# A sixth buffer for the x tiles of the last stage, and two work tiles with one buffer each

## The chip, the cores and the metric

The kernel runs on one core of one Trainium2 chip. The metric is the device time of one execution in microseconds (us), the median over runs. All data is float32.

## What is computed

Two bottleneck blocks of a residual network follow each other on an input of 64 images, 1024 channels, 14 x 14 pixels. Cut to what matters, one block is:

```python
out = relu(bn(conv1x1(x, w1, b1), g1, be1))      # 1024 -> 256 channels
out = relu(bn(conv3x3(out, w2, b2), g2, be2))    # 256 -> 256
out = bn(conv1x1(out, w3, b3), g3, be3)          # 256 -> 1024
out = relu(x + softplus(residual_scale)[0] * out)
```

`bn` takes mean and variance over all images and pixels of a channel, so a block can't be normalized before the whole of its convolution is known. The output of the first block is the `x` of the second.

## The kernel before

The activations between the convolutions (256 channels, all pixels) stay in SBUF as `y_all`. The 1024-channel tensor does not fit: it is cut into T = 32 tiles of two images, `[128, 8, 392]` float32, 1568 KB each, which travel between HBM and SBUF. The second block reads its x tiles from the DRAM tiles `mids`.

The stages run one after the other: first 1x1 convolution of block 0, its 3x3 convolution, a stage that fuses the last convolution of block 0 with the first of block 1, the 3x3 convolution of block 1, the Gram stage (products of `y` with itself, from which the statistics of the last convolution are computed before it runs), and the last stage, `final`. The change lies in the last one.

**The last stage.** Tile 0 is done by `residual` with plain products. Then `final` takes the tiles in pairs, t and t + 1 for t = 1, 3, ..., 29: 15 pairs. Tile 31 is done by `residual` again. A pair is 4 units (`q` = 0 to 3), and each unit makes two slots of 128 output channels for both tiles. A unit is a two by two block product done with seven products instead of eight (`Seven`, `Conv3Pair`): p1 to p7, each one product of a 128 x 128 weight and 392 columns, which the profile shows as two matmul instructions of L175. The sums that this needs of the operands, t1 to t4, are made once a pair by `column_sums` on DVE (L468 makes t3, L469 t2 = t3 + y, L470 t1, L471 t4 = y - t2). In the profile all four are named `ct`, in memory they are the tags ct0 to ct3. t1 is read by p5, t2 by p6, t3 by p7 and t4 by p4. Likewise the weights' sums are `ws`, and the plain weights `w`.

`stream` sets the order on PE. For each unit it issues p1 of this unit, p3 and p4 of the unit before, then p6, p2, p5 and p7 of this unit. So the unit before ends inside this one; at a pair's border p4 of the old pair still reads the old t4 after p1 of the new pair. PE and ACT instructions are held in program order; most of DVE's, POOL's and SP's are placed by the framework's scheduler, which hands out a buffer only when all readers of its former tile are done.

What the products make is drained so:

- p1, p6, p7 and p4 add up in one PSUM bank (`cy`). After p1, p6 and p7 ACT copies the bank's state, scaled, into SBUF (L338, named `cu`: twice into `cu12`, once into `cu3`), and the next product onto the bank waits for that copy.
- DVE adds the banks of p2, p5, p3 and p4 to the x tiles in place (L504). p5 and p3 add up in one bank (`cp`), so p3 waits for the add that follows p5. The add after p2 goes to the first tile of the pair, the one after p5 to the second.
- POOL adds `cu12` (L551, twice a unit) and `cu3` (L525, once a unit) to the x tiles.
- ACT does bias and relu on three of the unit's four parts (L338, `x<-x,shift`), DVE on the fourth (L560), and SP issues two stores for the unit (L563), when two more units have been begun.

Loads are issued by SP too (`load_x`, L129). Five tiles are loaded ahead of the stage: the pool `x_left` has five buffers, some of which serve the Gram stage as `homes` until it is over. In pair t, after its second unit, the loads up to tile t + 4 are requested; each waits until the stores of the tile that had its buffer have landed.

Of the kernel before, what the change touches and what calls it, by code (L numbers as in the profile page):

```python
# [38 lines left out]
FP = mybir.dt.float32  # L39
# [3 lines left out]
P = 128  # L43
# [6 lines left out]
T = N // G  # L50
PX = G * HW
# [39 lines left out]
def bottlenecks(ctx: ExitStack, tc: tile.TileContext, x, w1s, w2s, w3s, pars, out):  # L91
# [14 lines left out]
    def two(t, s):  # L106

        j = t % (GI // G)
        return y_grp[:, s, t // (GI // G), :, j * G * W : (j + 1) * G * W]

    class Psum:


        def __init__(self, scope, cycle, **bufs):
            self.pool = scope.enter_context(
                tc.tile_pool(name="psum", bufs=1, space=bass.MemoryType.PSUM, reuse_waits="tile")
            )
            self.cycle, self.bufs = itertools.cycle(cycle), bufs
# [5 lines left out]
    def load_x(pool, b, t, parts=1, run=lambda ins: None):  # L124
        xt = pool.tile([P, CS, PX], FP, tag="x", name=f"x_{b}_{t}")
        n = CS // parts
        for i in range(parts):
            run(
                nc.sync.dma_start(  # L129
                    out=xt[:, i * n : (i + 1) * n, :].rearrange("p s f -> p (s f)"),  # L130
                    in_=(x[t] if b == 0 else mids[t])[:, i * n * PX : (i + 1) * n * PX],
                )
            )
        return xt
# [12 lines left out]
    def sums_tile(pool, n):  # L147

        return pool.tile([P, n, 4 * CS // 2 * P], FP, tag="ws", name="ws")
# [14 lines left out]
    def combine_w3(w, s):  # L164
        n = CS // 2
        return combine([[w[:, k, o * n : (o + 1) * n] for k in range(MS)] for o in range(2)], s)

    def load_w3(pool, b):
        w = pool.tile([P, MS, CS, P], FP, tag="w3", name=f"w3_{b}")
        nc.sync.dma_start(out=w, in_=w3s[b])  # L170
        return w
# [168 lines left out]
    class Conv1(Seven):  # L340
# [89 lines left out]
        def run(self, ins, o, i):  # L430
            if self.pinned:
                tc.keep_in_program_order(ins)
# [25 lines left out]
        def after7(self):  # L458
            self.result(1, 1, self.p, self.saved("au3"))

    def column_sums(pool, ys, n):

        sums = []
        for i in range(4):
            v = pool.tile([P, n], FP, tag=f"ct{i}", name=f"ct{i}", bufs=2 if i > 1 else 1)
            sums.append(v.rearrange("p (h l) -> p h l", l=G * W))
        t1, t2, t3, t4 = sums
        nc.vector.tensor_sub(t3, ys[1][1], ys[0][1])  # L468
        nc.vector.tensor_add(t2, t3, ys[0][0])  # L469
        nc.vector.tensor_sub(t1, ys[0][1], ys[0][0])  # L470
        nc.vector.tensor_sub(t4, ys[1][0], t2)  # L471
        return sums

    class Conv3(Seven):

        prefix = "c"

        def __init__(self, psum, pool, xt, q, n, ys, sums, w3, aff, to):  # L480
            self.psum, self.pool, self.xt, self.n = psum, pool, xt, n
# [17 lines left out]
        def part(self, row, i):  # L499
            return self.xt[:, self.o[row], i * self.n : (i + 1) * self.n]  # L500
# [20 lines left out]
            self.add(1, 1, self.p)  # L521

        def after7(self):
            u3 = self.saved(self.pool.tile([P, self.n], FP, tag="cu3", name="cu3", bufs=2), 1)
            nc.gpsimd.tensor_add(self.part(1, 1), self.part(1, 1), u3)  # L525

        def after3(self):
# [12 lines left out]

    class Conv3Pair(Conv3):


        def part(self, row, i):
            return self.xt[i][:, self.o[row], :]
# [834 lines left out]
    def final(psum, pool, xpool, xs, a, w3, aff):  # L1380


        units = []

        def pairs():
            for t in range(1, T - 1, 2):
                ys = [[two(t + i, s) for i in range(2)] for s in range(MS)]
                sums = column_sums(pool, ys, PX)
                for q in range(CS // 2):
                    units.append(Conv3Pair(psum, pool, xs[t : t + 2], q, PX, ys, sums, w3, aff, out[t : t + 2]))  # L1390
                    yield units[-1]

                    while len(units) > 2:
                        units.pop(0).go_out()
                    if q == 1:

                        for i in range(len(xs), min(t + 5, T)):
                            xs.append(load_x(xpool, 1, i))

        for _ in stream(pairs(), (T // 2 - 1) * CS // 2):  # L1400
            pass
        for unit in units:
            unit.go_out()
        residual(psum, xs[T - 1], 1, T - 1, a, aff)
# [182 lines left out]
    def right_pool(name):  # L1587

        scope = ExitStack()
        return scope.enter_context(tc.tile_pool(name=name, bufs=2, side="right")), scope  # L1590

    x_right, x_scope = right_pool("first_x_right")
    with tc.tile_pool(name="first", bufs=1) as one, tc.tile_pool(
        name="first_x", bufs=2
    ) as x_left, ExitStack() as scope:
        xpools = x_right, x_left
        psum = Psum(scope, ["ps"], ps=4, ay=2)
# [37 lines left out]
    for b in range(2):  # L1635
        pb = par[b]
        minus_c = keep.tile([P, MS], FP, tag="minus_c", name="minus_c")
        nc.vector.tensor_scalar(minus_c, pb[:, BE2 : BE2 + MS], 0.0, -1.0, ALU.max, ALU.mult)
        stats2 = keep.tile([P, MS, 1 + PARTS, nc.vector.BN_STATS_DIM], FP, tag="stats2", name=f"stats2_{b}")
        with tc.tile_pool(name=f"conv2_{b}", bufs=1, reuse_waits="tile") as pool, ExitStack() as scope:  # L1640
            border.go_on(Psum(scope, ["l"], l=2, m=2), pool, stats2)

        if b == 0:
            x_right, x_scope = right_pool("last_x_right")
        with tc.tile_pool(name=f"last_{b}", bufs=1) as one, tc.tile_pool(
            name=f"last_x_{b}", bufs=2 if b == 0 else 5
        ) as x_left:
            xpools = (x_right, x_left) if b == 0 else (x_left, x_left)
            w3 = load_w3(one, b)
            if b == 0:  # L1650
                w1 = load_w1(one, b + 1, nc.sync)
            aff = affine(aggregate(stats2, 0), pb, G2, BE2)
            with ExitStack() as scope:
                if b == 0:
                    psum = Psum(scope, ["cy", "ay", "cx", "cy", "ay"], cy=2, ay=2)
                else:
                    psum = Psum(scope, ["cy", "cx"], cy=2, cx=2, cp=2)
                with tc.tile_pool(name=f"gram_{b}", bufs=1) as pool:
                    def x_tile(name, t=0):
                        return xpools[t].tile([P, CS * PX], FP, tag="x", name=name)  # L1660


                    ws = sums_tile(one, 2 - b)
                    homes = [x_tile("home"), x_tile("home") if b else ws.rearrange("p i n -> p (i n)"), x_tile("home", 1)]

                    made_c, made_a = [], []
                    beside = {NPX // (CH * P) - 10: lambda: made_c.append(combine_w3(w3, ws[:, 0]))}
                    if b == 0:
                        beside[NPX // (CH * P) - 4] = lambda: made_a.append(combine_w1(w1, ws[:, 1]))
                    grams = gram(psum, pool, homes, aff, minus_c, beside)  # L1670

                    made = [conv3(psum, 0, 0, w3, "cx" if b else "ay")]
                    mv3 = small.tile([P, CS, nc.vector.BN_AGGR_DIM], FP, tag="mv3", name="mv3")
                    conv3_stats(psum, pool, grams, w3, mv3, ("cy", "cp", "cy", "cp" if b else "cx"), homes[2])
                made.append(conv3(psum, 0, 1, w3, "cx" if b else "ay"))
                tags = ("cy", "cp") * 2 if b else ("cy", "cx", "cy")
                made += [conv3(psum, 0, 2 + i, w3, tag) for i, tag in enumerate(tags)]
                if b == 0:
                    psum.cycle = itertools.cycle(["ay", "ay", "cy"])
                aff = affine(mv3, pb, G3, BE3, conv_bias=B3)  # L1680
                for a in aff:
                    nc.vector.tensor_scalar(a, a, sps[b], None, ALU.mult)
                xs = [load_x(xpools[t % 2], b, t, run=tc.keep_in_program_order) for t in range(2 if b == 0 else 5)]
                later = None if b else []
                residual(psum, xs[0], b, 0, w3, aff, made, later)
                weights = made_a + made_c
                with tc.tile_pool(name=f"rest_{b}", bufs=1) as pool:
                    if b == 1:
                        final(psum, pool, x_left, xs, w3, *weights, aff)
                        return  # L1690
                    stats1 = stats_tile(MS, f"stats1_{b + 1}")
                    border = Border(b + 1, stats1, x_scope)
                    fused(psum, pool, xpools, xs, *weights, aff, par[b + 1], stats1, border, later)
# [40 lines left out]
```

## Time and profile before

| what | value |
|---|---|
| median of 3 runs | 1917.84 us (1916.82 to 1920.01) |
| the profiled execution | 1919.44 us |
| its span, first to last instruction | 1917.7 us |
| granted TensorE clock | 1.00 |
| DMA over the span | 213 GB/s |
| DMA from 1825 to 1850 us, inside the last stage | 357 GB/s, busy 0.97 |
| x tile loads of the second block | 32 of 1568 KB, median 8.6 us to landing |
| stores of the last stage | 392 KB mostly, median 5.6 us to landing |

In a row of a group or of the timeline stand the start and the duration, the engine, the line of the kernel, the operation, what it writes and reads by the program's names, and how often. An arrow in brackets tells how long the engine was idle before it and what ended that. PE is TensorE, PEld its weight loads, DVE VectorE, ACT ScalarE, POOL GpSimd, SP the queue that issues most DMAs. In the rows of stretches each engine has its busy time and, in brackets, its instructions; the last three numbers are the granted clock, the DMA busy share and GB/s.

### The profile page before, as it was taken

To read this page: it belongs to the slowest core of one execution; us is meant where nothing else is said; L and a number is where in the kernel's file an instruction comes from. 1 tells how busy PE (TensorE), PEld (TensorE's weight loads), DVE (VectorE), ACT (ScalarE), POOL (GpSimd) and SP (SyncE) were. 2 spreads that over 40 slices of the span, in tenths; PEclk is the share of its full clock that TensorE was granted. 3 is DMA by queue.
4 is the path that set the end of the run, shared out by engine and by line. 5 is a ranking of instruction groups with operands and counts; after the bars stand their busy time and mean duration, and the time that the engine had idled before them with its cause. 6 is when DMAs were issued, how large, how long until landed. Compare 5 with 4: busy or idle time off the path is not lost. (4 is left out here: it accounts for less than half of the span.)

```text
span 1917.7 us, 28725 instructions
## 1 busy us (share of the span) xinstructions
PE 1900.9 (99%) x10232; PEld 1598.3 (83%) x10232; DVE 1542.5 (80%) x2491; ACT 1086.1 (57%) x2160; POOL 572.6 (30%) x682
## 2 busy tenths in 40 slices
PE   9999999999999999999999999999999999999999
PEld 5555557999998899999999999989999986555555
DVE  5787767999998867677777767789999986888786
ACT  2222214677778255555555555557777692666665
POOL 0111100211205133333434334302121141666664
PEclk9999999999999999999999999999999999999999
DMA  7777644887946534444444444358788466899898
GB/s 286 275 248 279 216 155 152 210 215 208 220 165 172 205 147 169 169 173 184 177 173 168 168 173 178 125 180 218 213 208 224 146 162 251 290 327 346 312 338 300
DMA packets 198527, 408.77 MB, mean 213 GB/s; under 512 B 37104, under 2 KB 175024, under 8 KB 181872
## 3 DMA queue, kind: packets, MB, share of 16 engines
q1 hardware_dynamic: 159712, 321.85, 49.1%
q0 software_dynamic: 33056, 34.03, 8.6%
q10 hardware_dynamic: 5616, 51.06, 6.4%
q8 instruction: 81, 1.33, 0.3%
q14 instruction: 62, 0.51, 0.1%
HBM read 263.75 MB, written 115.34 MB: 198 GB/s over the span
## 5 line engine op out<-in xcount | busy, mean ns | idle before, releaser
L338 ACT ACTIVATE cu<-cy,scale 128x196 f32<-128x196 f32 (+1 forms) x552 | 256.3, 473 | 280.9 <-PE cy L175 275.7
L175 PE MATMUL columns<-v,ub 128*128 128x224 f32 (+1 forms) x1536 | 302.3, 338 | 2.0 <-ACT columns L846 1.0
L338 ACT ACTIVATE x<-x,shift 128x392 f32<-128x392 f32 x452 | 255.0, 613 | 72.8 <-POOL x L530 53.6
L175 PEld LDWEIGHTS columns<-v,ub 128*128 128x128 f32 x1536 | 269.0, 188 | 7.4 <-ACT columns L846 2.2
L504 DVE SCALAR_TENSOR_TENSOR x<-cp,scale,x 128x196 f32<-128x196 f32 (+1 forms) x368 | 178.0, 484 | 100.1 <-PE cp L175 96.3
L175 PE MATMUL cy<-ct,ws 128*128 128x196 f32 (+1 forms) x736 | 221.8, 383 | 1.2 <-ACT cu L338 1.2
L175 PE MATMUL ay<-at,ws 128*128 128x196 f32 (+1 forms) x768 | 212.8, 382 | 0.0
L525 POOL TENSOR_TENSOR x<-x,cu 128x196 f32<-128x196 f32 (+1 forms) x184 | 160.1, 870 | 172.8 <-ACT cu L338 163.7
L530 POOL TENSOR_TENSOR x<-x,cu 128x392 f32<-128x392 f32 x124 | 125.9, 1015 | 191.4 <-DVE x L504 191.4
L175 PEld LDWEIGHTS ay<-at,ws 128*128 128x128 f32 x768 | 139.3, 190 | 34.7 <-issue 0.2
L175 PEld LDWEIGHTS cy<-ct,ws 128*128 128x128 f32 x736 | 133.4, 190 | 36.4 <-ACT cu L338 3.7
L175 PE MATMUL l<-diffs,ub 128*128 128x224 f32 (+1 forms) x768 | 149.6, 337 | 0.3 <-ACT sd L1476 0.3
L551 POOL TENSOR_TENSOR x<-x,cu 128x392 f32<-128x392 f32 x120 | 121.9, 1017 | 87.5 <-DVE x L504 69.1
L175 PE MATMUL m<-sums,ua 128*128 128x224 f32 (+1 forms) x752 | 146.0, 336 | 0.2 <-DVE sums L667 0.2
L338 ACT ACTIVATE au<-ay 128x196 f32<-128x196 f32 (+1 forms) x140 | 53.3, 381 | 152.8 <-PE ay L175 150.0
L175 PEld LDWEIGHTS l<-diffs,ub 128*128 128x128 f32 x768 | 134.6, 189 | 1.2 <-ACT sd L1476 0.6
L504 DVE SCALAR_TENSOR_TENSOR x<-cx,scale,x 128x196 f32<-128x196 f32 (+1 forms) x184 | 89.1, 484 | 56.7 <-PE cx L175 56.7
L175 PEld LDWEIGHTS m<-sums,ua 128*128 128x128 f32 x752 | 131.4, 189 | 1.4 <-DVE sums L667 0.8
L175 PE MATMUL cy<-y,w 128*128 128x196 f32 (+1 forms) x408 | 125.3, 393 | 0.0
L175 PE MATMUL cx<-y,w 128*128 128x196 f32 (+1 forms) x400 | 122.7, 392 | 0.0
L175 PE MATMUL cp<-y,ws 128*128 128x196 f32 (+1 forms) x368 | 113.6, 390 | 2.5 <-DVE x L504 2.5
L175 PE MATMUL cy<-ct,w 128*128 128x196 f32 (+1 forms) x368 | 110.9, 383 | 0.5 <-ACT cu L338 0.5
(238 smaller groups left out, 3918.0 us busy)
## 6 DMA issues: line engine op xcount, KB each, us to landing
x<-in_x SPq DMA_DIRECT2D x62, 1568.0 KB, 6.9
ub<-u SPq DMA_DIRECT2D x92, 768.0 KB, 5.3
x<-mid SPq DMA_DIRECT2D x32, 1568.0 KB, 8.6
mid<-x ACTq DMA_DIRECT2D x31, 1568.0 KB, 5.1
out<-x SPq DMA_DIRECT2D x123, 392.0 KB, 5.6
ua<-u SPq DMA_DIRECT2D x92, 256.0 KB, 3.1
u<-y POOLq DMA_DIRECT2D x48, 256.0 KB, 5.5
home<-y SPq DMA_DIRECT2D x70, 96.0 KB, 3.5
```

The source lines that it names most:

```text
L175: tc.keep_in_program_order(nc.tensor.matmul(*args, **kw))
L338: tc.keep_in_program_order(nc.scalar.activation(*args, **kw))
L504: nc.vector.scalar_tensor_tensor(v, bank, self.scale[:, o : o + 1], v, ALU.mult, ALU.add)
L525: nc.gpsimd.tensor_add(self.part(1, 1), self.part(1, 1), u3)
L530: nc.gpsimd.tensor_add(v, v, self.u12)
L551: nc.gpsimd.tensor_add(v, v, self.u12[:, i * self.n : (i + 1) * self.n])
```

## The change

The last stage gets a sixth buffer for x tiles, `last_more`, in the place that the Gram stage has left. The sixth tile (tile 5) is loaded into it ahead of the stage, behind the other five; from then on every sixth tile uses it. In pair t the loads up to tile t + 5 are requested in place of t + 4. To make room, t4 and `cu3` of the last stage have one buffer in place of two (`twice`, `thirds`); t3 keeps two. The fused stage, which uses the same functions, keeps its buffers.

```diff
-    def column_sums(pool, ys, n):
+    def column_sums(pool, ys, n, twice=(2, 3)):
...
-            v = pool.tile([P, n], FP, tag=f"ct{i}", name=f"ct{i}", bufs=2 if i > 1 else 1)
+            v = pool.tile([P, n], FP, tag=f"ct{i}", name=f"ct{i}", bufs=1 + (i in twice))
...
     class Conv3(Seven):
+        thirds = 2
...
-            u3 = self.saved(self.pool.tile([P, self.n], FP, tag="cu3", name="cu3", bufs=2), 1)
+            u3 = self.saved(self.pool.tile([P, self.n], FP, tag="cu3", name="cu3", bufs=self.thirds), 1)
...
     class Conv3Pair(Conv3):
+        thirds = 1
...
     def final(psum, pool, xpool, xs, a, w3, aff):
-                sums = column_sums(pool, ys, PX)
+                sums = column_sums(pool, ys, PX, (2,))
...
-                        for i in range(len(xs), min(t + 5, T)):
-                            xs.append(load_x(xpool, 1, i))
+                        for i in range(len(xs), min(t + len(xpool), T)):
+                            xs.append(load_x(xpool[i % len(xpool)], 1, i))
...
+                if b == 1:
+                    more = scope.enter_context(tc.tile_pool(name="last_more", bufs=1, reuse_waits="tile"))
+                    xs.append(load_x(more, b, len(xs), run=tc.keep_in_program_order))
                 with tc.tile_pool(name=f"rest_{b}", bufs=1) as pool:
                     if b == 1:
-                        final(psum, pool, x_left, xs, w3, *weights, aff)
+                        final(psum, pool, [x_left] * 5 + [more], xs, w3, *weights, aff)
```

## The prediction

> **What bounds the kernel now.** I read the page first, then the stretches of the last stage, the waits of DVE there, the timeline around one wait and around one pair border, and last SP's timeline. The page:
>
> ```profile
> span 1917.7 us, 28725 instructions
> PE 1900.9 (99%) x10232; PEld 1598.3 (83%) x10232; DVE 1542.5 (80%) x2491; ACT 1086.1 (57%) x2160; POOL 572.6 (30%) x682
> ...
> PE 31%; DMA 2%; DVE 1%; ACT 0%; issue 0%; DVEq 0%; SPq 0%; ACTq 0%
> ```
>
> TensorE is full; the change takes no work from it, so it can win only idle PE time, and only in the last stage (from about 1617 us). The stretches say how little that is, and that the transfers are nearly full too:
>
> ```profile
> 1750.00:1775.00 25.00, 25.00 (x76) 13.79 (x75) 21.18 (x33) 16.45 (x32) 16.61 (x17) 1.00 0.98 349
> 1775.00:1800.00 25.00, 23.45 (x71) 13.06 (x70) 18.59 (x29) 15.81 (x31) 15.36 (x15) 1.00 0.87 306
> ```
>
> The second column is PE: 1.55 us are missing after 1775. The waits of DVE from 1634 to 1900 us, and the timeline at the longest, name the cause:
>
> ```profile
> DVE x L504 <- DMA x<-mid: 2.8, 4, 1.6
> ```
>
> ```profile
> 1788.97 0.82 PE L175 MATMUL cp<-ct,ws 128*128 128x392 f32 x2
> ...
> 1790.29 0.82 PE L175 MATMUL cy<-y,w 128*128 128x392 f32 x2
> ...
> 1791.99 0.62 DVE L504 SCALAR_TENSOR_TENSOR x<-cp,scale,x 128x392 f32<-128x392 f32 x1 [1.59 <-DMA x<-mid]
> ...
> 1792.67 0.93 PE L175 MATMUL cp<-y,ws 128*128 128x392 f32 x2 [1.55 <-DVE x L504]
> ```
>
> The add after p5 needs the second x tile of its pair, which has not landed; p3 accumulates on the same bank and waits for the add. SP shows why the tile is late: each group of two loads waits for the stores that free its buffers, and stands in one queue with eight stores.
>
> ```profile
> 1761.80 2.72 SPq L129 DMA_DIRECT2D x<-mid  x2
> 1764.57 17.77 SPq L563 DMA_DIRECT2D out<-x  x8
> 1782.51 1.06 SPq L129 DMA_DIRECT2D x<-mid  x2
> 1783.62 19.20 SPq L563 DMA_DIRECT2D out<-x  x8
> 1803.45 1.35 SPq L129 DMA_DIRECT2D x<-mid  x2
> ```
>
> Load groups come 20.7 and 20.9 us apart here, while PE takes 18.8 us for a pair when it is not held. The group of 1782.51 carries as its first tile the second tile of the very next pair: landed at 1791.8 (the chain of waits has 9.26 us for it), due at 1789.8, where p5 ends.
>
> A second, smaller loss recurs at each pair border, where DVE makes the next pair's operand sums:
>
> ```profile
> 1708.45 0.82 DVE L469 TENSOR_TENSOR ct<-ct,y 128x392 f32<-128x392 f32 x1
> ...
> 1709.31 0.57 DVE L471 TENSOR_TENSOR ct<-y,ct 128x392 f32<-128x392 f32 x1
> ...
> 1711.00 0.93 PE L175 MATMUL cp<-y,ws 128*128 128x392 f32 x2
> ...
> 1711.72 1.37 DVE L470 TENSOR_TENSOR ct<-y 128x392 f32<-128x392 f32 x1
> ...
> 1713.01 0.55 DVE L468 TENSOR_TENSOR ct<-y 128x392 f32<-128x392 f32 x1
> ...
> 1715.09 0.61 DVE L504 SCALAR_TENSOR_TENSOR x<-cp,scale,x 128x392 f32<-128x392 f32 x1
> ...
> 1715.76 0.93 PE L175 MATMUL cp<-y,ws 128*128 128x392 f32 x2
> ```
>
> From 1708.45 to 1716.54 DVE has no idle. Both p3 start late, by 0.12 and 0.04 us, and each costs another 0.105 us since its second weights are then loaded late (second matmul 0.434 us after the first; 0.329 undisturbed): 0.37 us a border, 5.2 us over 14 borders.
>
> **The change, part by part.**
>
> *Sixth x buffer.* No instruction is added; 32 loads stay 32. At pair t the loads still wait for the stores of tiles t-2 and t-1, but bring tiles t+4 and t+5, not t+3 and t+4. Tile t+3 was the one due in the very next pair; now every load has a further pair, 18.8 us. What it removes, as p1-to-p3 start against 0.70 us at an undisturbed border (1715.06 to 1715.76): 2.38 - 0.70 = 1.68 us at 1790; 1810.77 to 1811.89 is 1.12, so 0.42 at 1811; 1867.62 to 1869.05 is 1.43, so 0.73 at 1868. Sum 2.8 us, all on PE's path. The next thing due behind each is the border itself, already counted. Nor should lateness catch up: from the group of 1685.27 to that of 1880.19 ten intervals average 19.5 us, so a group loses 0.7 us a pair against PE, some 8 us over twelve pairs, under the 18.8 gained. Even at 20.9 throughout it would be 25 us, against 18.8 and the 3 us the early groups had in hand; only the last pairs could then stall.
>
> Here a rule stands against the change. The Trainium skill (DMA: Bandwidth & Descriptors, Specifications) gives about 358 GB/s between HBM and a core. A pair moves four tiles of 1.605 MB: 6.42 MB, 17.9 us at that rate, less than PE's 18.8. By it the transfers keep up and a buffer buys nothing: sum 0. The stretch above does move 349 GB/s, so the rate is right; but the trace's intervals of 20.7 and 20.9 us contain waits that no rate has, and I follow the rows: 2.8 us.
>
> *Its early load.* It follows the fifth on SP, which issues at 1607.73, so about 1608.1. Two queued loads land 4.5 to 5 us apart, so about 1619. DMA is 0.19 busy from 1612 to 1618, and no store stands behind it on SP before 1631. If that cover went, tile 0's store (POOL, 1618.58, 5.4 us) would be later by at most one load, 5 us, with nobody waiting for it but tile 6's load. Cost 0. In return the last group has one load less.
>
> *One buffer for cu3.* ACT's next cu3 must wait for POOL's L525. That ends at 1702.92 for a cu3 begun at 1701.26; the next begins at 1705.87, 2.95 us later (3.1 at the border). Cost 0. Without that cover ACT would hold its later reads of the y bank, which p1 and p6 already wait on by fractions of a microsecond, and PE would pay one for one.
>
> *One buffer for t4.* L471, now at 1709.31, may start only when p4 of the old pair's last unit has read the old t4: 1712.59. It is due at the next p4, about 1716.4. Count stays 15, so nothing is added by its own row of 0.57 us; it moves out of the first half of the dense stretch into the second. Worked through: without it the first p3 is on time (gain 0.23); the ops behind it come 0.4 us earlier until L468; then it goes in and the add after p5 is where it was, 1715.1 or 0.1 later. So 0 at the second p3, which sets the border's end; 0 to +0.1 us a border. The new wait is DVE on PE; queued behind are the adds of p3, p4, p2 and p5, for which POOL, ACT and PE wait.
>
> The trace has no L471 in the new place. Nearest row for the price there: L470, two SBUF inputs like it, 1.37 us where POOL was running, against 0.55 for L468 where POOL was idle. The skill's rule (SBUF — State Buffer, SBUF: two separate sides) says a DVE op with two SBUF inputs and a GpSimd op lock each other out, the earlier one for its whole length. POOL runs from 1714.18 to 1716.32. By L471's present row the border costs 0; by the rule, if the L551 of 1714.18 is ahead of it, up to 0.8 us, times 14 = 11 us. From below: were it placed after the add of p5, both p3 would be on time, -0.37 us times 14 = -5.2. I take 0: directly behind p4 it stands ahead of that POOL op.
>
> *Sum.* The profiled execution took 1919.44 us (span 1917.7 and 1.7 around it): 1919.4 - 2.8 = 1916.6. The median of the runs is 1917.84, 1.6 below it; as the stalls follow from an order fixed in the program, I take them to be in those runs too: 1915.0.
>
> **The rivals.**
> *Slower: t4 behind POOL.* If L471 lands after the add of p4 in DVE's order, at about 1714.2, the L551 begun just before holds it for 0.7 to 0.8 us, and the add of p5, with no slack, goes with it: 0.75 times 14 = 10.5, less 2.8: 1925.5. It decides as soon as L471 sits between POOL's first L551 after the border and the add of p5. For: L470's 1.37. Against: p4 ends before that POOL op starts.
> *Faster by more: the border loosens.* L471 lands where the add of p5 no longer waits for it: half to all of 5.2 us more, 1912.4 to 1909.8. For: the first p3 is surely freed. Against: t4 is due by 1716.4, so it can't go far back.
> *Nothing: the lateness returns.* The queue stays the slower one at 20.9 us, late tiles move to later pairs, or the stalls in the runs are smaller than in the profile: 1917 to 1918.
>
> **How the numbers follow.** Likeliest 0.42 (its own range 1913.5 to 1916.6), slower 0.23, faster by more 0.22, nothing 0.13. A difference under 0.2%, 3.8 us, is about what a measurement of this kernel can't tell from none; below 1914.0 counts as faster, above 1921.7 as slower. Faster: 0.22 and 0.11 from the lower edge of the likeliest, 0.33. Slower: 0.23, with 0.01 from the first. The range leaves out the outer tails: 1910 to 1924.
>
> **What would show it.** Right: no wait of DVE L504 for x<-mid after 1634; six loads before the first L563; p3 at borders late by under 0.4 us together; L471 at 0.5 to 0.6 us behind the add of p3. Wrong: L471 at 0.8 us or more with p3 later than now; an ACT wait for POOL L525; a rest of waits for x<-mid in the last pairs.

## The result

Over 21 runs each the changed kernel takes 1915.12 us (1913.89 to 1916.89), the kernel before 1919.38 us (1916.82 to 1921.44) on the same chips: ratio 0.9980, 95% interval 0.9974 to 0.9987, or 4.3 us less. The profiled execution took 1915.46 us, with a span of 1913.7; the one of before, 1919.44 and 1917.7. (Behind the new lines of code the old L504, L525, L551, L560 and L563 are L505, L526, L553, L562 and L565. The edits of some experiments shift them again: there DVE's adds are L509, and a row's operation and names tell what it is.)

The page of the changed kernel: TensorE's work is the same, the span is 4.0 us shorter, and the chain of waits no longer breaks off at transfers of x tiles.

```profile
span 1913.7 us, 28716 instructions
PE 1899.4 (99%) x10232; PEld 1600.8 (84%) x10232; DVE 1542.1 (81%) x2491; ACT 1087.0 (57%) x2160; POOL 581.8 (30%) x682
...
PE 97%; ACT 1%; DVE 1%; issue 0%; DMA 0%; POOL 0%; SPq 0%; DVEq 0%; ACTq 0%; POOLq 0%
```

The waits of DVE from 1634 to 1896 us, all of them: none is for x<-mid.

```profile
DVE x L505 <- PE cp L175: 21.2, 43, 0.7
DVE x L505 <- PE cx L175: 19.6, 29, 0.7
```

In the stretches PE is full where it lacked 1.55 us, and the transfers are as full as in the first of the two stretches before (349 GB/s):

```profile
1750.00:1775.00 25.00, 25.00 (x76) 13.95 (x75) 21.09 (x34) 16.77 (x32) 17.44 (x17) 1.00 0.98 352
1775.00:1800.00 25.00, 25.00 (x77) 14.23 (x76) 20.58 (x32) 17.62 (x34) 17.02 (x16) 1.00 0.99 352
```

SP's timeline: seven issues stand in the first row, the five tiles, the sixth behind them, and tile 6 in the place where tile 5 was; the load groups then come 18 to 19 us apart in this stretch.

```profile
1584.61 40.46 SPq L129 DMA_DIRECT2D x<-mid  x7
...
1764.17 1.29 SPq L129 DMA_DIRECT2D x<-mid  x2
1765.51 16.51 SPq L565 DMA_DIRECT2D out<-x  x8
1782.19 1.32 SPq L129 DMA_DIRECT2D x<-mid  x2
1783.56 17.15 SPq L565 DMA_DIRECT2D out<-x  x8
1800.87 1.05 SPq L129 DMA_DIRECT2D x<-mid  x2
```

And a pair border in the timeline:

```profile
1708.41 0.82 PE L175 MATMUL cx<-y,w 128*128 128x392 f32 x2
1708.61 0.83 DVE L469 TENSOR_TENSOR ct<-ct,y 128x392 f32<-128x392 f32 x1
1709.36 0.61 DVE L505 SCALAR_TENSOR_TENSOR x<-cx,scale,x 128x392 f32<-128x392 f32 x1
...
1711.04 0.82 PE L175 MATMUL cp<-y,ws 128*128 128x392 f32 x2
1711.28 0.55 DVE L470 TENSOR_TENSOR ct<-y 128x392 f32<-128x392 f32 x1
1711.76 1.37 DVE L468 TENSOR_TENSOR ct<-y 128x392 f32<-128x392 f32 x1
1713.05 0.61 DVE L505 SCALAR_TENSOR_TENSOR x<-cp,scale,x 128x392 f32<-128x392 f32 x1
1713.59 0.55 DVE L471 TENSOR_TENSOR ct<-y,ct 128x392 f32<-128x392 f32 x1
1713.74 1.27 POOL L553 TENSOR_TENSOR x<-x,cu 128x392 f32<-128x392 f32 x1 [1.04 <-DVE x L505]
...
1715.13 0.61 DVE L505 SCALAR_TENSOR_TENSOR x<-cp,scale,x 128x392 f32<-128x392 f32 x1
```

L471 now stands behind the add of p3, ahead of the POOL op; that op takes 1.27 us in place of about 1.02, as it waits for L471. The first p3 (1711.04) is on time, 0.66 us behind p1; the second is 0.15 us late. With the late second weights a border costs PE 0.25 us, and did cost 0.37.

**The accounts of PE.** Take the starts of all matmuls of the last stage and sum what each lies later than 0.329 us behind the one before, where it is over 0.03 us. Before: 9.3 us; after: 4.7. Of the first, 2.8 are late loads, 5.1 borders, and 1.4 the stage's beginning and end. Of the second, 0 are late loads, 3.3 borders and 1.4 the ends. That is 4.6 us less; the span won 4.0, since in this execution the stage began 0.65 us later.

### The profile page after: what moved, and what is told of

Same layout as the page of the kernel before. It is cut to its first block, busy times and chain, and to the rows that moved or that the text cites. A ratio compares the mean times of both kernels' runs of the same rounds, so it can differ in the third digit from the quotient of the medians.

```text
span 1913.7 us, 28716 instructions
## 1 busy us (share of the span) xinstructions
PE 1899.4 (99%) x10232; PEld 1600.8 (84%) x10232; DVE 1542.1 (81%) x2491; ACT 1087.0 (57%) x2160; POOL 581.8 (30%) x682
## 4 chain that ended last, share of the span: by engine, by line
PE 97%; ACT 1%; DVE 1%; issue 0%; DMA 0%; POOL 0%; SPq 0%; DVEq 0%; ACTq 0%; POOLq 0%
PE ay L175 18%; PE cy L175 18%; PE columns L175 15%; PE cp L175 12%; PE ap L175 11%; PE m L175 7%; PE l L175 7%; PE cx L175 5%; PE ax L175 4%; PE ps L175 1%; DMA x<-in_x 0%; PE cx L1207 0%; ACT columns L848 0%; PE cy L1207 0%; ACT x L338 0%
## 5 line engine op out<-in xcount | busy, mean ns | idle before, releaser
L505 DVE SCALAR_TENSOR_TENSOR x<-cp,scale,x 128x196 f32<-128x196 f32 (+1 forms) x368 | 178.2, 484 | 96.2 <-PE cp L175 95.0
L526 POOL TENSOR_TENSOR x<-x,cu 128x196 f32<-128x196 f32 (+1 forms) x184 | 165.8, 901 | 172.6 <-ACT cu L338 163.9
L531 POOL TENSOR_TENSOR x<-x,cu 128x392 f32<-128x392 f32 x124 | 125.9, 1015 | 191.2 <-DVE x L505 191.2
L553 POOL TENSOR_TENSOR x<-x,cu 128x392 f32<-128x392 f32 x120 | 125.8, 1049 | 73.7 <-DVE x L505 72.8
L505 DVE SCALAR_TENSOR_TENSOR x<-cx,scale,x 128x196 f32<-128x196 f32 (+1 forms) x184 | 89.0, 484 | 57.0 <-PE cx L175 57.0
```

The lines of the kernel that those rows point to most:

```text
L505: nc.vector.scalar_tensor_tensor(v, bank, self.scale[:, o : o + 1], v, ALU.mult, ALU.add)
L531: nc.gpsimd.tensor_add(v, v, self.u12)
L553: nc.gpsimd.tensor_add(v, v, self.u12[:, i * self.n : (i + 1) * self.n])
```

## The experiments

The theory, formed from these two traces: the gain has two parts. Late loads go because of the sixth buffer (2.8 us in the profiled execution), and borders get cheaper by 0.12 us because L471 moves (1.8 us over the stage). The rivals: the sixth buffer is all of it; the place of L471 doesn't matter, or it could be worse; the lateness is a full queue that no buffer mends.

### The work tiles alone, with five x buffers

```diff
-                if b == 1:
-                    more = scope.enter_context(tc.tile_pool(name="last_more", bufs=1, reuse_waits="tile"))
-                    xs.append(load_x(more, b, len(xs), run=tc.keep_in_program_order))
...
-                        for i in range(len(xs), min(t + len(xpool), T)):
+                        for i in range(len(xs), min(t + 5, T)):
```

> Five x buffers as before, t4 and cu3 with one buffer each. Theory (the change has two parts: late loads 2.8 us, and 0.12 us a border from moving L471): the first p3 of each border is on time, p1 to p3 start 0.66 us there, the second p3 late by some 0.15 us; the waits of DVE for x<-mid stay at 2.8 us or grow to 5, since PE is faster and the loads are not. Time against before: -1.6 us from the borders, 0 to +1.6 back in waits, so 1917.8 to 1919.4 where before is 1919.4. Rival (the sixth buffer is all of it, the borders only look different): both p3 as late as before, 0.37 us a border, time 1919.4.

Measured: 1916.3 us against 1918.8, ratio 0.9989 (0.9980 to 0.9998). The borders are those of the changed kernel: first p3 on time, second 0.15 us late. So the borders' part is real and comes without the buffer. The late loads came back, but smaller than I had expected. The waits of DVE in this kernel:

```profile
DVE x L505 <- DMA x<-mid: 1.3, 3, 0.5
```

At two borders p1 to p3 is 0.40 and 0.54 us longer than at the others: 0.9 us, not 2.8. (At the last border, where the changed kernel loses nothing, p3 and its second weights are late by 0.2 us more: 1.1 us in all.)

### The kernel before, a second trace

No edit.

> The kernel before, a second trace. Theory: the late loads follow from the fixed order on SP, so the waits of DVE for x<-mid come again at 2.8 us, give or take 0.5, at the same three borders. Rival (they are the luck of a run): some other sum, between 0.5 and 4 us, at other borders.

Measured, in this one execution: 1918.5 us. The theory's number fell. Two borders are late, by 0.34 and 0.96 us, 1.3 us in all, at about 1810 and 1867; the one at 1790, with 1.68 the largest of the first trace, is on time. So the lateness is of the place (it comes in the same stretch, at borders that the first trace had too), its size is of the run. The waits list only 0.2 us for x<-mid here, since the largest stands under another name:

```profile
1867.44 0.63 DVE L504 SCALAR_TENSOR_TENSOR x<-cp,scale,x 128x392 f32<-128x392 f32 x1 [0.86 <-PE cy L175]
```

An add of a `cp` bank has nothing to wait for in `cy`, and its tile landed at 1867.22, 0.2 us ahead of it: it is the load.

### cu3 with two buffers again

On the kernel before, with its five x buffers, t4 alone gets one buffer:

```diff
-    def column_sums(pool, ys, n):
+    def column_sums(pool, ys, n, twice=(2, 3)):
...
-            v = pool.tile([P, n], FP, tag=f"ct{i}", name=f"ct{i}", bufs=2 if i > 1 else 1)
+            v = pool.tile([P, n], FP, tag=f"ct{i}", name=f"ct{i}", bufs=1 + (i in twice))
...
-                sums = column_sums(pool, ys, PX)
+                sums = column_sums(pool, ys, PX, (2,))
```

So it differs from the first experiment by cu3 alone.

> Five x buffers, t4 with one buffer, cu3 with two as before: differs from the first experiment by cu3 alone. Theory (ACT never waits for L525, the slack is 3 us): the same as the first experiment, ratio to before 0.999, no wait of ACT cu for POOL in either. Rival (cu3 with one buffer holds ACT now and then): faster than the first experiment by over 1 us.

Measured: 1916.31 us against 1918.26, ratio 0.9992 (0.9983 to 1.0001); the first experiment had 0.9989. ACT waits for no POOL op ahead of a `cu` in either. No cost of the single cu3 shows. Three borders are late in this trace, by 1.6 us together.

### t4 one place later: behind the add of p4

```diff
-        nc.vector.tensor_sub(t4, ys[1][0], t2)
+        fourth = lambda: nc.vector.tensor_sub(t4, ys[1][0], t2)
...
+            later.append(lambda: tc.keep_in_program_order(fourth()))
...
+        def after4(self):
+            super().after4()
+            self.then4()
...
+                    units[-1].then4 = later[0]
```

The old pair's last unit makes t4 of the next pair, behind its add of p4.

> The changed kernel with L471 held behind the add of p4 on DVE, one place later. Theory (POOL and DVE shut each other out, whichever begins first): L471 meets the L553 that POOL has begun and takes 1.2 to 1.4 us in place of 0.55; the add of p5 and the second p3 come 0.7 to 0.8 us later at 14 borders: +10 us on the changed kernel, about 1925. Rival (the place of L471 doesn't matter as long as it is ahead of p4): L471 0.55 us, 1915.

Measured: 1921.85 us against 1918.8, ratio 1.0017 (1.0008 to 1.0026): slower than before, and 6.7 us slower than the changed kernel, with no late load. The timeline at a border:

```profile
1715.43 1.03 POOL L566 TENSOR_TENSOR x<-x,cu 128x392 f32<-128x392 f32 x1 [1.04 <-DVE x L509]
1715.81 1.07 DVE L471 TENSOR_TENSOR ct<-y,ct 128x392 f32<-128x392 f32 x1
1716.80 0.61 DVE L509 SCALAR_TENSOR_TENSOR x<-cx,scale,x 128x392 f32<-128x392 f32 x1
1717.34 0.61 DVE L509 SCALAR_TENSOR_TENSOR x<-cp,scale,x 128x392 f32<-128x392 f32 x1
```

The POOL op is ahead by 0.38 us, and L471 takes 1.07 us in place of 0.55, ending 0.42 us behind it. The second p3 is 0.67 us late, 0.52 more than in the changed kernel; times 13 that is 6.8 us. The slower rival of the prediction was a true mechanism, one place in DVE's order away. I had its price at 0.7 to 0.8 us, since I let L471 meet the POOL op sooner after its start. And it was held for 0.52 us where 0.65 us of the POOL op were left, so a little less than by the rule that the prediction cites.

### t4 behind the add of p5

The same edit, with `after5` of the new pair's first unit.

> The changed kernel with L471 held behind the add of p5. Theory: the second p3 is on time (-0.25 us a border), but L471 waits for POOL's L553 until 1.0 to 1.4 us after its start, and the p4 that reads t4 starts 0.3 to 0.6 us late: +1 to +4 us on the changed kernel, about 1917.5. Rival (t4 is not due so early): p4 on time, -3.3 us, 1911.9.

Measured: 1915.44 us against 1918.8, ratio 0.9984 (0.9975 to 0.9993), the time of the changed kernel. L471 takes 1.12 us, as expected, and the second p3 is on time:

```profile
1714.42 1.12 DVE L471 TENSOR_TENSOR ct<-y,ct 128x392 f32<-128x392 f32 x1
1715.65 0.30 PEld L175 LDWEIGHTS cy<-ct,w 128*128 128x128 f32 x2 [0.58 <-ACT cu L338]
```

The second row is the weight load of p4. The bracket names a copy of ACT's, but at every border the load starts 0.12 us behind L471's end, so it is t4 that it waits for. p4 is late by 0.15 us only, not 0.3 to 0.6: with its late second weights 0.22 us a border, where the changed kernel has 0.25. At the borders next to nothing is won by it: the delay goes from p3 to p4.

### t4 behind the add of p2, in the kernel before

```diff
-        nc.vector.tensor_sub(t4, ys[1][0], t2)
+        with tc.issue_after(behind.ins) if behind is not None else ExitStack():
+            nc.vector.tensor_sub(t4, ys[1][0], t2)
```

with `behind` the add of p2 of the old pair's last unit. Five x buffers, two buffers for t4 and cu3.

> The kernel before, with five x buffers and two buffers for t4 and cu3, but L471 held one place back, behind the add of p2. Theory (the 0.12 us a border that the change won are the start of L471: directly behind L469, whose t2 it reads, it starts 0.86 us after it, where an add that does not read t2 starts after 0.75): with an add between the two the dense chain is 0.1 us shorter and the border costs PE 0.26 us, not 0.37, though L471 stays in the first half: -1.5 us against before. Rival (the gain comes of L471 leaving the first half): the border stays at 0.37 us, no gain.

Measured: 1915.8 us against 1918.26, ratio 0.9986 (0.9976 to 0.9995). L471, here L472, stays in the first half, and the border still gets cheaper, from 0.37 to 0.10 us. So L471 need not leave the first half for the border to get cheaper. The rows show where the gain lies:

```profile
1707.90 0.83 DVE L469 TENSOR_TENSOR ct<-ct,y 128x392 f32<-128x392 f32 x1
1708.65 0.61 DVE L505 SCALAR_TENSOR_TENSOR x<-cx,scale,x 128x392 f32<-128x392 f32 x1
1709.19 0.55 DVE L472 TENSOR_TENSOR ct<-y,ct 128x392 f32<-128x392 f32 x1
1709.66 0.61 DVE L505 SCALAR_TENSOR_TENSOR x<-cp,scale,x 128x392 f32<-128x392 f32 x1
1710.20 0.64 DVE L561 TENSOR_SCALAR x<-x,shift 128x392 f32<-128x392 f32 x1
...
1709.41 1.21 POOL L552 TENSOR_TENSOR x<-x,cu 128x392 f32<-128x392 f32 x1 [1.10 <-DVE x L505]
```

In the kernel before, L469 started at 1708.45, and then:

```profile
1710.56 1.02 POOL L551 TENSOR_TENSOR x<-x,cu 128x392 f32<-128x392 f32 x1 [1.71 <-DVE x L504]
1710.87 0.93 DVE L560 TENSOR_SCALAR x<-x,shift 128x392 f32<-128x392 f32 x1
```

From L469 to L561 it is 2.30 us; before it was 2.42. This 0.12 is the theory's: what comes next starts 0.75 us behind L469 when it does not read its result, 0.86 when it does. (That the next op is a sum and not an add isn't the reason: L472 starts 0.54 us behind an add, as the add at 1710.33 in the kernel before did behind another, 0.53.) The rest is more than I had expected: L561 takes 0.64 us and not 0.93, as POOL began its op earlier (the add of p2, which releases it, comes 0.6 us sooner after L469), so less of it is left to wait for. The late loads in this trace are 2.2 us, late second weights counted in.

### t3 out of the border

t3 of the next pair is made in the middle of the pair instead of at the border, on the changed kernel:

```diff
+        def third_of(t):
+            v = pool.tile([P, PX], FP, tag="ct2", name="ct2", bufs=2)
...
+            tc.keep_in_program_order(nc.vector.tensor_sub(v, two(t + 1, 1), two(t + 1, 0)))
...
                     if q == 1:
+                        third = third_of(t + 2) if t + 2 < T - 1 else None
```

> The changed kernel with t3 of the next pair (L468, 1.37 us at the border because POOL runs) made in the middle of the pair, behind the DVE instruction that follows its second unit's request. Theory (what is left of the border is DVE's dense chain): both p3 on time, PE loses nothing at the border: 0.25 us by 13 is -3.3 us, 1911.9. Rival (the wait for POOL only moves: adds in the middle of the pair come late and hold p3 there): no gain, 1915, or slower.

Measured: 1912.64 us (1911.6 to 1913.63) against 1918.8, ratio 0.9968 (0.9956 to 0.9981). Every run is below every run of the changed kernel. By the sum of starts PE loses 1.4 us in the whole stage, its two ends; at no border is a p3 late. t3 takes 0.55 us in the middle of the pair (here L1394), since the DVE op ahead of it has just waited for POOL:

```profile
1699.67 0.81 DVE L566 TENSOR_SCALAR x<-x,shift 128x392 f32<-128x392 f32 x1
1700.40 0.55 DVE L1394 TENSOR_TENSOR ct<-y 128x392 f32<-128x392 f32 x1
1701.11 0.62 DVE L509 SCALAR_TENSOR_TENSOR x<-cp,scale,x 128x392 f32<-128x392 f32 x1 [0.15 <-PE cp L175]
```

The bracket in the last row is the point: DVE has idle time left here, so nothing waits for t3. This version beats both kernels.

### The same with five x buffers

```diff
-                    more = scope.enter_context(tc.tile_pool(name="last_more", bufs=1, reuse_waits="tile"))
-                    xs.append(load_x(more, b, len(xs), run=tc.keep_in_program_order))
...
-                        final(psum, pool, [x_left] * 5 + [more], xs, w3, *weights, aff)
+                        final(psum, pool, [x_left] * 5, xs, w3, *weights, aff)
```

> As the kernel with t3 in the middle of the pair, but with five x buffers: it differs from that one by the sixth buffer alone. Theory (the sixth buffer takes lateness of loads off PE, and the faster PE is, the more of it there is): DVE waits for x<-mid, and PE loses 2 to 5 us by them: 1914.6 to 1917.6 where the kernel with six has 1912.6. Rival (the lateness came from the borders, a border without delay has none): no waits, 1912.6.

Measured: 1914.67 us (1911.55 to 1916.87) against 1918.49, ratio 0.9976 (0.9967 to 0.9985). Between this kernel and the last only the sixth buffer differs: 2.0 us by the medians, 1.5 by the ratios, whose intervals overlap. Its waits of DVE:

```profile
DVE x L509 <- DMA x<-mid: 4.3, 5, 1.7
```

PE loses 0.5, 0.3, 1.2 and 0.1 us at four borders, and 0.1 each by late weights: 2.5 us. With no other delay at the borders the loads are still late, so the borders were not their cause.

### t3 by POOL

```diff
-        nc.vector.tensor_sub(t3, ys[1][1], ys[0][1])
+        by.tensor_sub(t3, ys[1][1], ys[0][1])
...
-                sums = column_sums(pool, ys, PX, (2,))
+                sums = column_sums(pool, ys, PX, (2,), nc.gpsimd if t > 1 else nc.vector)
```

> The changed kernel with t3 (L468) of all pairs but the first made by POOL. Theory: DVE's dense chain at the border loses 1.37 us and both p3 are on time as with t3 in the middle of the pair, but POOL has 1.0 us more at the border, and L526 and L553 and ACT's relu behind them come later: -3.3 us for the p3, up to +2 back by ACT: 1912 to 1914. Rival (POOL's extra op holds the lock against L470 and L471): no gain, 1915 or later.

Measured: 1912.82 us against 1918.49, ratio 0.9972 (0.9961 to 0.9982). Both p3 are on time at every border, but for second weights 0.07 us late. L470 takes 1.37 us and L471 0.84 as they wait for POOL, so the rival's lock is there; but without L468 the chain is short enough to bear it.

### Six buffers, loads requested as before

```diff
-                        for i in range(len(xs), min(t + len(xpool), T)):
+                        for i in range(len(xs), min(t + len(xpool) - 1, T)):
```

> The changed kernel with its six buffers, but loads requested only up to tile t + 4 as before: each load finds a buffer that has been free for a pair and waits for no store of the pair before. Theory (lateness came from the wait for stores, a queue turn of store and load): no DVE wait for x<-mid either, as a load group is issued about 9 us after the pair's start and lands well ahead of its due time 23 us after it: same as the changed kernel, 1915. Rival (the queue is simply full and any load behind eight stores is late): waits of 1 to 3 us return, 1916 to 1918.

Measured: 1916.08 us against 1918.49, ratio 0.9988 (0.9979 to 0.9997); the changed kernel's interval, 0.9974 to 0.9987, overlaps it. No wait for x<-mid stands in its list, and from the fourth pair on each pair's second tile landed 3.4 us or more ahead of its add; so loads that stand in the queue behind eight stores need not be late. But what I wrote of it was half wrong: only one tile of a group finds a free buffer, the other still waits for a store of the pair before (the load at 1763.48 starts 0.02 us after such a store has landed). The median is 1 us above the changed kernel's; its PE account is 5.0 us against 4.7, 0.3 of it at one border. The rest I can't tell from noise.

## Why the prediction was right, and where it was not

The time, 1915.0 forecast and 1915.12 measured, and the likeliest case hold. Not all terms do.

- **Late loads, -2.8.** The mechanism is shown: six traces with five buffers have late loads at two to four borders (2.8, 1.3, 1.1, 1.6, 2.2 and 2.5 us), six with six buffers have none. The size is not: 2.8 was the largest of the six. I took the sum of one execution to be in every run, "as the stalls follow from an order fixed in the program". The order is fixed, the moment of landing is not. Two pairs of kernels differ by the buffer alone: the medians give 2.0 us (1914.67 to 1912.64) and 1.2 (1916.3 to 1915.12), the ratios 1.5 and 1.7, and in both pairs the intervals overlap. So its gain is shown by the traces, and its size is known only roughly.
- **The rate of 358 GB/s** (the Trainium skill, DMA: Bandwidth & Descriptors, Specifications) would have said 0. As an average it fits (352 GB/s in the stretches after), though it is no ceiling here: one slice of 10 us in the trace of before shows 384. What it leaves out is the due time. In the first trace of before, the second tile of a pair landed 4.1 us ahead of its add in the fourth pair and 2.3 in the ninth; from the tenth on it is 0.1 to 1.1 us, and four of these six adds waited for it. In the changed kernel the same tile landed 17.6 us ahead in the fourth pair and 12.3 in the last. So the buffer bought most of a pair's time, and the rest of the stage used 5.3 us of it (the prediction had some 8).
- **The border, 0 to +0.1 each.** This term failed. It was -0.12 each, -1.8 us in all. I counted L471 with its own 0.57 us in both places and let the add of p5 be "where it was". But directly behind L469 it cost 0.11 more, as its start waits for L469's result; and I kept POOL's position fixed while DVE's moved.
- **The rival of the POOL lock** was 0.52 us a border in its experiment rather than 0.75, and did not come in the changed kernel, because DVE's order put L471 directly behind the add of p3 and ahead of the POOL op, as forecast.
- **The early load and cu3, 0 each.** The sixth load was issued at 1608.75 and landed at 1618.62 (forecast 1608.1 and 1619), and nobody waited; cu3 is shown by its own experiment.
- **The end of the sum.** 1919.4 less 2.8 and 1.8 is 1914.8; the profiled execution took 1915.46, the stage having begun 0.65 us later. The three runs of before on which the prediction leaned have a median 1.5 us under that of the 21 runs, 1919.38: the step from 1916.6 down to 1915.0 was not needed. The missing gain at the borders (1.8 us) and that step (1.6) made up for each other by luck, so the forecast is closer than its terms.

What stays open: why lateness is 1.1 us in one execution and 2.8 in another; and whether the sixth buffer asked for early (up to t + 5) is better than asked for late, for which the two intervals are too wide.

## What to carry to other kernels

A buffer more is worth what the waits for late tiles cost on the engine that bounds, no more, and one trace shows one draw of them: take two traces before you size it. When the transfers are as fast as the rate allows and tiles still come late, look at which transfer each load waits for and when its data is due; a tile needed one step later can cost nothing where one needed now costs a microsecond. And where an engine is busy without a gap for a few microseconds around a border, take out of that stretch what has a later due time: moving one sum, 1.37 us at the border with its wait for POOL and 0.55 in the middle of the pair, won 2.5 us, more than half of what the whole change did.

## What the runs showed of the hardware

- Of a DVE sum of two SBUF operands and a POOL op that meet, the one that began later took longer. L471 took 0.55 us ahead of a POOL op (which then took 1.27 in place of 1.02), and 1.07 us when it began 0.38 us behind one. The adds that read a PSUM bank took 0.61 to 0.63 us beside POOL and alone.
- A DVE op that reads what the one just before it has written starts later: 0.86 us behind L469 against 0.75 for one that doesn't, though L469 takes 0.82 us in both.
- A product that had to wait costs PE about 0.1 us beyond the wait: its second weights are then loaded late, and its second matmul comes 0.434 us behind the first, not 0.329.
